# A causal attention block: a score moved within its step, row maxima split in SBUF, some adds on VectorE and part of W1's sums moved into attention

## The chip, the cores and the metric

The kernel runs on one core of one Trainium2 chip. The time is that of the device for one execution, in microseconds (us), as the median of several runs. The hardware profiler records one further execution. The profile names the engines PE (TensorE: matmuls), PEld (its weight loads), DVE (VectorE), ACT (ScalarE), POOL (GpSimd) and SP (SyncE, which here issues most DMAs). "L204" is line 204 of the kernel's file.

## The reference

One block of a diffusion transformer in fp32, for x of 2 x 2048 x 512 and 16 heads of 32 channels:

```python
mod = silu(condition) @ Wada + bada            # shift, scale, gate, for attention and MLP
xm = layernorm(x, g1, be1) * (1 + sc_a) + sh_a
scores = einsum('bhqd,bhkd->bhqk', q, k) * hd ** -0.5
attn = softmax(where(causal, scores, -inf))
x = x + gt_a * ((attn @ v) @ Wproj + bproj)
xm = layernorm(x, g2, be2) * (1 + sc_m) + sh_m
x = x + gt_m * (gelu(xm @ W1 + b1) @ W2 + b2)
```

## The kernel before

The two batches run one after the other. For each there is a QKV phase, an attention phase and a projection; the MLP for both comes last. On the profile's time axis: start and QKV of batch 0 from 0 to 202.4, attention 0 to 734.1, projection 0 to 790, QKV of batch 1 to 972.8, attention 1 to 1500.4, projection 1 to 1559.8, MLP to 2278.1.

**Units and steps.** Attention is cut into 16 units per batch, in the list `units`: a group c of four heads (`HC` = 4, together 128 channels) times a block i of 512 queries (`QB`). A unit has 4 i + 3 steps: a step takes one tile of 128 keys against the 512 queries, and the last two steps hold the diagonal's shorter tiles, so that they are narrow (under 512 wide).

**Maxima first.** Every score is computed twice. First in natural layout (queries on partitions): `bank` (line 463) makes one matmul of 128 queries by up to 512 keys, into a tile called s; DVE then takes its row maximum into mx, by a plain reduction (L484) or, at the diagonal, with the causal mask (L479, followed by a small read of an accumulator). The tiles of s come from a PSUM pool of two banks. When the last score of a unit is out, `split` (line 487) turns the unit's maxima into three bf16 parts, mhl, in five small DVE operations (L501 to L505); the maximum itself and a remainder are kept in the columns of the PSUM tile of the last score. `rows` (line 539) transposes mhl on PE (ps_m, also in a bank of the s pool) and DVE spreads it into fold (L549).

**Then the step.** `scores_t` (line 578) starts the four heads' transposed scores st (keys on partitions) in four further PSUM banks, each with a matmul of sel and fold, which puts minus the maximum there, and adds the product of keys and queries. ACT takes the exponential into e (L620), POOL zeroes what lies above the diagonal (affine_select, L629). Two steps later (`LAG` = 2) PE makes the products o of e and the values vv. For the row sums sm, the e of four steps are first added up by POOL in chains (L650, `add`, line 648), so that PE needs one product with ones for four steps; in the last unit of a batch DVE adds.

**What sets the order.** The scores in natural layout belong to units up to three ahead (`AHEAD`) and wait in `row.todo`. For each step `due` and `count` work out from costs how many, n, are to be issued; `scores_t` places them among the transposed scores: with n over 4 one ahead of the first head, one behind heads 0 and 2 each, one in a bank of the st pool behind head 3, and one more; what is over goes behind the step's products. The order of PE, of ACT's exponentials and of POOL is that of the code (`mm` and `act` keep it); DVE's reductions and the loads may be moved by a scheduler. The pending products are issued by `flush`, which in the last unit stands behind `row.prepare`: that is the step's share of work for the projection, with a matmul ps_rows that turns rows of the gate.

**Loads.** Keys kst and queries qst go to DRAM and come back in another layout; `asked` (line 879) asks for the first ones of a group of tokens in the QKV phase, keys first, on SP's queue.

**Weights.** The MLP's matrices are multiplied by a scheme with seven products in place of eight, at two levels, so W1 and W2 need sums of their blocks, which POOL makes ahead of time. The class `Quarters` makes the 16 pieces of the first level: eight in QKV of batch 0, eight in attention 0 (with `beside` and `among`, line 1150: loads and stores on SP's queue, the sums, L1135, in steps of the diagonal, where POOL has no adds). `FirstLayer` makes W1's second level in QKV of batch 1: seven pieces, each with a load of 1 MB and a store on POOL's own queue and four sums (L1196).

**End of the projection.** `inv_std` (line 222) takes a square root on ACT (rstd2) for the second layernorm behind the last statistics, for either batch. The MLP's matmuls ps_a and ps_b, and ACT's copies c (L1877), follow.

Of the kernel before, what the change touches and what calls it, by code (L numbers as in the profile page):

```python
# [17 lines left out]
P = 128  # L18
# [9 lines left out]
def dit_block_kernel(  # L28
# [283 lines left out]
    class Row:  # L312
# [174 lines left out]
        def split(self, u, mx, s):  # L487

            hl = mhl[u % (AHEAD + 1)][:, :, : 4 * TQ].rearrange(
                "p h (t l) -> p h t l", l=4
            )
            mx = mx.rearrange("p (h t) n -> p h t n", h=HC)
            m, rest = [
                s[:, n * HC * TQ : (n + 1) * HC * TQ].rearrange("p (h t) -> p h t", h=HC)
                for n in range(2)
            ]  # L500
            nc.vector.tensor_reduce(m, mx, axis=AX.X, op=ALU.max)  # L501
            nc.vector.tensor_reduce(hl[:, :, :, 0], mx, axis=AX.X, op=ALU.max)
            nc.vector.tensor_tensor(rest, m, hl[:, :, :, 0], ALU.subtract)
            nc.vector.tensor_tensor(hl[:, :, :, 1], m, hl[:, :, :, 0], ALU.subtract)
            nc.vector.tensor_tensor(hl[:, :, :, 2], rest, hl[:, :, :, 1], ALU.subtract)  # L505
# [11 lines left out]
        def score(self, n, borrow=None):  # L517

            for k in range(n):
                if borrow and k % 2 == 0:
                    s = borrow()
                else:
                    s = ps_sp.tile([P, QB], F32, tag="s", name="s")
                item = self.todo.pop(0)
                u = item[0]
                if self.mx is None:
                    self.mx = bp.tile(  # L530
                        [P, HC * TQ, units[u][1] + 1], F32, tag="mx", name="mx", bufs=3
                    )
                self.bank(*item, s)
                if not self.todo or self.todo[0][0] != u:
                    self.split(u, self.mx, s)
                    self.mx = None
                    self.at += 1
# [26 lines left out]
    def attention_phase(row, beside=None):  # L564
        b, vv, kst, qst = row.b, row.vv, row.kst, row.qst
        with pool(f"att{b}") as ap, pool(
# [7 lines left out]
            def scores_t(u, step, n):  # L574
# [73 lines left out]
            def add(u, dst, x, y):  # L648
                engine = nc.vector if u == len(units) - 1 else nc.gpsimd
# [61 lines left out]
            for u, (c, i) in enumerate(units):  # L711
# [5 lines left out]
                for n_step, tiles in enumerate(steps_of[u]):  # L717
# [82 lines left out]
    class Qkv:  # L800
# [46 lines left out]
        def group(self, g, hp, between, among):  # L847
# [31 lines left out]
            def asked():  # L879
                row.load_keys(0, g)  # L880
                row.load_queries(g)
# [219 lines left out]
    class Quarters:  # L1101
# [8 lines left out]

        def load(self, room, queue=nc.gpsimd):
# [38 lines left out]
        def beside(self, pool_):  # L1150
# [4 lines left out]
            def among(now, slack, last):  # L1155
                if not todo and self.at < FC:
                    todo.extend([(now + 3, "load"), *((now + 6, n) for n in range(4))])
                    if now == 0:
                        todo[0] = (0, "load")
# [5 lines left out]
                if what == "load":  # L1165
                    todo.pop(0)
                    self.load(room, nc.sync)
                    todo[:] = [(now + 3, n) for n in range(4)]
                elif what == "store":
                    todo.pop(0)  # L1170
                    self.store(nc.sync)
                elif slack or last:
                    todo.pop(0)
                    self.make((what,))
# [3 lines left out]
            return among  # L1178

# [25 lines left out]
    class FirstLayer:  # L1205
# [20 lines left out]
        def store(self):  # L1226

            act(nc.gpsimd.dma_start(w1e[self.stored], self.rooms[self.stored % 2]))
            self.stored += 1

    def project_phase(row, psum, between):
# [59 lines left out]
        lo, hi = b * NT, (b + 1) * NT  # L1291
        inv_std(mv2, rstd2, lo, hi, shift2)
# [147 lines left out]
    attention_phase(row, quarters.beside)  # L1440
# [4 lines left out]
    with pool("qkv1") as qp, pool("ps_qkv1", bufs=6, space=PSUM) as ps_mm:  # L1445
# [20 lines left out]
        with pool("hl1") as hp:  # L1466
# [14 lines left out]
            late_loads = range(1, 43, 6)  # L1481
            qkv.run(hp, also)
            assert late.stored == 7

    attention_phase(row)
# [6 lines left out]
    with ExitStack() as mlp:  # L1492
# [692 lines left out]
```

## Time and profile before

| | us |
|---|---|
| median of 3 runs | 2277.54 (2277.3 to 2277.65) |
| profiled execution | 2279.83 |
| its span | 2278.1 |
| PE busy | 2238.0 (98%) |
| DVE busy | 1556.9 (68%) |
| POOL busy | 1317.1 (58%) |
| ACT busy | 980.2 (43%) |
| busiest DVE group: reductions L484 of s | 409.2 in 606 |
| busiest POOL group: adds L650 to a chain | 498.6 in 212 |

The span is the time between the first and the last instruction that the profiler shows. The table of busy times gives the sum over all phases; an engine that is idle for half of the kernel can still be the one that everything waits for in a stretch. A row of the waits lists what one engine waited for, as it can be inferred from semaphores. A row of the groups by line ends with the idle time of the engine ahead of the group's instructions. A row of the timeline has the start, the duration, the engine, the line, the operation with its output and inputs, how many were put together (x2), and in brackets the idle time before and what ended it.

### The profile page before, as it was taken

Reading aid. Unit: us, or ns where it says so; the run is one execution under the profiler, and the core shown is the slowest. Engines: PE = TensorE matmul, PEld = TensorE weight load, DVE = VectorE, ACT = ScalarE, POOL = GpSimd, SP = SyncE. Lnnn points to the kernel's source line nnn. Section 1 sums busy time; section 2 is a strip of 40 time slices with the busy share of each in tenths; the row PEclk is TensorE's granted clock in tenths of the full one; section 3 lists DMA queues with packets and bytes.
Section 4 is the critical chain, followed back from the end, with each engine's and each line's share of the span. In section 5 each row is a group of like instructions: output and inputs, shape, how many; then the busy total and the mean of one; then the engine's idle time right before and its main releaser. Section 6 shows DMA issues by size and latency. Waiting matters only on the chain. (4 is left out here: it accounts for less than half of the span.)

```text
span 2278.1 us, 34363 instructions
## 1 busy us (share of the span) xinstructions
PE 2238.0 (98%) x12429; PEld 1439.8 (63%) x12429; DVE 1556.9 (68%) x3132; ACT 980.2 (43%) x1908; POOL 1317.1 (58%) x1052
## 2 busy tenths in 40 slices
PE   8999999999999999999999999999999999999999
PEld 3676455455544457754555545446888888888887
DVE  3467777777766525677777777555896876877787
ACT  3334555555566134355555555632332242251231
POOL 4362987888894553258788887554764602602510
PEclk9999999999999999999999999999999999999999
DMA  8869226262244778860511404265375654654643
GB/s 272 250 209 249 50 52 156 55 146 73 56 153 148 240 245 295 266 149 24 120 44 46 104 24 136 85 224 202 117 278 203 212 180 151 214 176 153 221 144 120
DMA packets 134147, 355.66 MB, mean 156 GB/s; under 512 B 14497, under 2 KB 33485, under 8 KB 119257
## 3 DMA queue, kind: packets, MB, share of 16 engines
q1 hardware_dynamic: 126112, 305.18, 45.1%
q0 software_dynamic: 7488, 47.74, 5.8%
q8 instruction: 98, 1.61, 0.3%
q14 instruction: 73, 0.59, 0.1%
q10 hardware_dynamic: 376, 0.55, 0.1%
HBM read 253.80 MB, written 107.48 MB: 159 GB/s over the span
## 5 line engine op out<-in xcount | busy, mean ns | idle before, releaser
L620 ACT ACTIVATE e<-st 128x512 f32<-128x512 f32 (+1 forms) x1152 | 572.9, 579 | 404.6 <-PE st L204 347.6
L484 DVE TENSOR_REDUCE mx<-s 128x1 f32<-128x512 f32 x606 | 409.2, 687 | 193.0 <-PE s L204 191.1
L650 POOL TENSOR_TENSOR ee<-ee,e 128x1024 f32<-128x1024 f32 x212 | 498.6, 2383 | 8.1 <-ACT e L620 8.1
L204 PE MATMUL s<-kst,qst 128*128 128x512 f32 (+3 forms) x1028 | 439.0, 430 | 15.1 <-DVE mx L484 8.6
L204 PE MATMUL st<-qst,kst 128*128 128x512 f32 (+3 forms) x1280 | 400.6, 377 | 0.0
L204 PE MATMUL ps_a<-sum,room 128*128 128x256 f32 x1504 | 356.8, 381 | 4.4 <-DVE c L1655 1.5
L204 PEld LDWEIGHTS ps_a<-sum,room 128*128 128x128 f32 x1504 | 280.8, 190 | 53.8 <-issue 6.0
L204 PE MATMUL o<-e,vv 128*32 128x512 f32 (+3 forms) x2560 | 302.9, 538 | 1.7 <-POOL e L629 1.7
L479 DVE CUSTOM_DVE_ANT_0 junk<-s,causal 128x512 bf16<-128x512 f32 (+3 forms) x422 | 206.7, 490 | 114.9 <-PE s L204 107.1
L204 PEld LDWEIGHTS s<-kst,qst 128*128 128x128 f32 x1028 | 193.3, 188 | 137.1 <-issue 44.3
L204 PEld LDWEIGHTS st<-qst,kst 128*128 128x128 f32 x1280 | 229.0, 188 | 63.2 <-issue 33.9
L650 POOL TENSOR_TENSOR ee<-e 128x1024 f32<-128x1024 f32 x84 | 198.2, 2382 | 112.1 <-ACT e L620 112.0
L629 POOL TENSOR_SCALAR_AFFINE_SELECT e<-e 128x256 f32<-128x256 f32 x256 | 103.8, 435 | 125.7 <-ACT e L620 124.2
L204 PEld LDWEIGHTS <-sel 32*128 32x128 bf16 x1152 | 29.2, 91 | 190.0 <-issue 188.0
L1883 POOL TENSOR_TENSOR c<-c,h 128x512 f32<-128x512 f32 x40 | 58.5, 1484 | 154.6 <-ACT c L1881 154.6
L204 PE MATMUL ps_b<-sum,room 128*128 128x256 f32 x608 | 143.6, 379 | 0.0
L204 PEld LDWEIGHTS o<-e,vv 128*32 128x32 f32 x2560 | 62.5, 108 | 100.8 <-issue 80.6
L204 PEld LDWEIGHTS ps_b<-sum,room 128*128 128x128 f32 x608 | 115.0, 190 | 15.4
L204 PE MATMUL ps_v<-wqkv,xmT 128*128 128x512 f32 x256 | 124.7, 600 | 0.0
L204 PE MATMUL st<-fold,sel 32*128 32x512 bf16 (+1 forms) x1152 | 115.3, 372 | 2.6 <-DVE mhl L505 1.2
L484 DVE TENSOR_REDUCE mx<-st 128x1 f32<-128x512 f32 x162 | 111.0, 685 | 2.9 <-PE st L204 0.6
L1528 POOL TENSOR_TENSOR sum<-xm 128x256 f32<-128x256 f32 x16 | 15.5, 972 | 152.8 <-PE ps_a L204 152.8
(236 smaller groups left out, 3276.5 us busy)
## 6 DMA issues: line engine op xcount, KB each, us to landing
qst<-q SPq DMA_DIRECT2D x128, 256.0 KB
room<-w1e SPq DMA_DIRECT2D x28, 1024.0 KB
kst<-k SPq DMA_DIRECT2D x24, 1024.0 KB
room<-w1e SPq DMA_DIRECT2D x28, 768.0 KB
room<-w2e SPq DMA_DIRECT2D x21, 1024.0 KB
q<-hl SPq DMA_DIRECT2D x32, 512.0 KB
k<-hl SPq DMA_DIRECT2D x32, 512.0 KB
room<-w2e SPq DMA_DIRECT2D x21, 768.0 KB
```

Of the source, the lines that this page charges most:

```text
L204: return tc.keep_in_program_order(nc.tensor.matmul(*args, **kw))
L479: nc.vector.tensor_tensor_reduce(junk[:, :w], s[:, :w], causal[:, QB - w :], 1.0, MASKED, ALU.add, ALU.max, m,)
L484: nc.vector.tensor_reduce(m, s[:, :w], axis=AX.X, op=ALU.max)
L620: act(nc.scalar.activation(e[:, h % 2, :w], sts[h][:, :w], AF.Exp))
L629: nc.gpsimd.affine_select(d, d, pattern=[[0, 2], [1, P]], compare_op=ALU.is_ge, fill=0.0, base=0, channel_multiplier=-1,)
L650: act(engine.tensor_tensor(dst, x, y, ALU.add))
L1528: act(engine.tensor_tensor(dst, x, y, ALU.subtract))
L1883: nc.gpsimd.tensor_tensor(c, c, piece_of(base, i, t, pair), ALU.add)
```

## The change

1. In a step with more than four scores that is 512 wide (and not in the first unit), the third score goes behind the fourth transposed score, ahead of the one in the st bank. In narrow steps, and in the first unit, it goes behind the one in the st bank.
2. `split` keeps its parts in an SBUF tile and works in six DVE operations, all reductions, in place of five. It no longer touches the last score's bank.
3. `add` takes DVE as soon as no score is left to do in the batch, in place of in the last unit alone.
4. In the last unit the pending products are issued ahead of `row.prepare`.
5. `asked` asks for queries ahead of keys.
6. Only three of W1's seven second-level pieces are made in QKV of batch 1. The other four are made in attention 1, as eight halves: the new class `FirstHalves` with 32 sums of 128x256, eight loads of 0.5 MB and eight stores on SP's queue, placed by `beside` as W2's are in attention 0.
7. Batch 1's `inv_std` is called in the MLP (first block, k = 3); at its old place stands a small square root.

```diff
-        def split(self, u, mx, s):
+        def split(self, u, mx):
...
-            m, rest = [
-                s[:, n * HC * TQ : (n + 1) * HC * TQ].rearrange("p (h t) -> p h t", h=HC)
-                for n in range(2)
-            ]
-            nc.vector.tensor_reduce(m, mx, axis=AX.X, op=ALU.max)
+            parts = bp.tile([P, HC, TQ, 3], F32, tag="parts", name="parts")
+            nc.vector.tensor_reduce(parts[:, :, :, 0], mx, axis=AX.X, op=ALU.max)
             nc.vector.tensor_reduce(hl[:, :, :, 0], mx, axis=AX.X, op=ALU.max)
-            nc.vector.tensor_tensor(rest, m, hl[:, :, :, 0], ALU.subtract)
-            nc.vector.tensor_tensor(hl[:, :, :, 1], m, hl[:, :, :, 0], ALU.subtract)
-            nc.vector.tensor_tensor(hl[:, :, :, 2], rest, hl[:, :, :, 1], ALU.subtract)
+            for n in range(1, 3):
+                nc.vector.tensor_reduce(
+                    parts[:, :, :, n], hl[:, :, :, n - 1 : n],
+                    axis=AX.X, op=ALU.max, negate=True,
+                )
+                with nc.allow_low_precision("sums of exact parts, rounded when written"):
+                    nc.vector.tensor_reduce(
+                        hl[:, :, :, n], parts[:, :, :, : n + 1], axis=AX.X, op=ALU.add
+                    )
...
-                after = (0, 2) if n > HC else (0, 1)
+                narrow = w < QB or u == 0
...
-                    if h in after and n >= 3 or h >= HC - n and n < 3:
+                    if h < 1 + (n <= HC) and n >= 3 or h >= HC - n and n < 3:
                         row.score(1)
+                if n > HC and not narrow:
+                    row.score(1)
                 if n >= 3:
                     row.score(1, st_bank)
-                    row.score(min(n, HC) - 3)
+                if n > HC and narrow:
+                    row.score(1)
+                if n > 3:
+                    row.score(1)
...
             def add(u, dst, x, y):
-                engine = nc.vector if u == len(units) - 1 else nc.gpsimd
+                engine = nc.gpsimd if row.todo else nc.vector
...
                     row.inverses(u, n_step)
+                    flush(now)
                     if u == len(units) - 1:
                         row.prepare(n_step)
-                    flush(now)
...
             def asked():
+                row.load_queries(g)
                 row.load_keys(0, g)
-                row.load_queries(g)
...
+    class FirstHalves:
...
+        def load(self, room, queue):
+            n, half = self.at // 2, self.at % 2
+            self.at += 1
+            w = room.rearrange("p (n d) -> p n d", n=7)
+            src = w1d[:, n].rearrange("p k (i f) d -> p (k i) (f d)", i=2)
+            act(queue.dma_start(w[:, 2:6], src[:, :, half * 2 * P : (half + 1) * 2 * P]))
+            self.loaded.append((n, half, w))
...
+                room_sum(self.loaded[0][2], 1, step)
...
+            act(queue.dma_start(w1e[n][:, :, half * 2 * P : (half + 1) * 2 * P], w))
...
-        lo, hi = b * NT, (b + 1) * NT
-        inv_std(mv2, rstd2, lo, hi, shift2)
+        if b + 1 < B:
+            inv_std(mv2, rstd2, 0, NT, shift2)
+        else:
+            act(nc.scalar.activation(first, eps, AF.Sqrt))
...
-            late_loads = range(1, 43, 6)
+            late_loads = range(1, 19, 6)
...
-    attention_phase(row)
+    halves = FirstHalves(late.stored)
+    attention_phase(row, beside(halves))
...
             def among(at, k):
+                if (m, at, k) == (0, 0, 3):
+                    inv_std(mv2, rstd2, NT, B * NT, shift2)
```

More of the change, by code (lines that the diff above doesn't have):

```diff
@@ L1148, in store, with beside, start @@
             )
-        def beside(self, pool_):
+    def beside(pieces):
+        def start(pool_):
             room = pool_.tile([P, piece], F32, tag="w7", name="w7")
@@ L1155, in among @@
             def among(now, slack, last):
[L1156 to L1159, printed above, removed]
+                if not todo and pieces.left():
+                    todo.append((now + 3 if now else 0, "load"))
                 elif not todo:
```

26 lines of the change are left out of this document (20 added, 6 removed).

## Prediction

> **What bounds the kernel now.** I read first the table of stretches, cut at the borders of the phases: from, to, length, then the busy time and count of PE, PEld, DVE, ACT and POOL. The second and the fourth stretch of the kernel, attention of batch 0 and of batch 1, matter most here:
>
> ```profile
> 202.40:734.10 531.70, 522.08 (x3682) 263.79 (x3681) 373.61 (x893) 303.33 (x608) 426.52 (x313) 1.00 0.40 103
> ...
> 972.80:1500.40 527.60, 519.57 (x3681) 262.71 (x3680) 373.47 (x893) 302.95 (x607) 404.37 (x281) 1.00 0.32 81
> ```
>
> PE is busy for 98% of both, at a granted clock of 1.00. DVE is busy for 70%, POOL for 80% and 77%. So PE's own sequence is the time, and the change, which leaves the count and the shapes of the matmuls alone, can only win what PE waits. Next come PE's waits, in attention 0 and then in attention 1 (total us, times, longest):
>
> ```profile
> PE s L204 <- DVE mx L484: 5.2, 8, 0.9
> PE o L204 <- POOL e L629: 1.3, 2, 1.1
> PE s L204 <- DVE mx L479: 0.9, 3, 0.4
> PE st L204 <- DVE mhl L505: 0.6, 1, 0.6
> PE ps_rows L204 <- ACT e L620: 0.5, 1, 0.5
> ```
> ```profile
> PE s L204 <- DVE mx L484: 3.4, 6, 0.9
> PE s L204 <- DVE mhl L505: 2.0, 4, 0.6
> PE st L204 <- DVE mhl L505: 0.6, 1, 0.6
> ...
> PE ps_rows L204 <- ACT e L620: 0.5, 1, 0.5
> PE o L204 <- POOL e L629: 0.5, 1, 0.5
> PE s L204 <- DVE mx L479: 0.2, 1, 0.2
> ```
>
> Scores wait 22 times for a maximum or for the split: 5.2 + 0.9 + 3.4 + 2.0 + 0.2 = 11.7 us. These rows are the pool from which the change can draw. The timeline of one such place (start, duration, then the instruction, in brackets the idle time before it) shows how it comes about and that the rows show too little:
>
> ```profile
> 1224.51 0.40 PE L204 MATMUL st<-qst,kst 128*128 128x512 f32 x1
> ...
> 1224.72 0.68 DVE L484 TENSOR_REDUCE mx<-s 128x1 f32<-128x512 f32 x1
> ...
> 1225.32 0.18 DVE L505 TENSOR_TENSOR mhl<-s,mhl 128x16 bf16<-128x16 f32 x1
> 1225.45 0.33 PE L204 MATMUL s<-kst,qst 128*128 128x128 f32 x1 [0.55 <-DVE mx L484]
> ```
>
> The split's L505 still reads a PSUM bank of the s pool. PE's next score into that bank starts at 1225.45, as L505 ends. It is named after L484, but L505 is the last to end. The row says 0.55; the starts are 1225.45 - 1224.51 = 0.94 apart.
>
> The usual distance of two starts is in the next fence, with the first and the last of the third scores of which part 2 speaks:
>
> ```profile
> 203.90 0.40 PE L204 MATMUL s<-kst,qst 128*128 128x512 f32 x1
> 204.13 0.62 PE L204 MATMUL st<-qst,kst 128*128 128x512 f32 x2
> 204.62 0.50 PE L204 MATMUL s<-kst,qst 128*128 128x512 f32 x1
> 204.95 0.40 PE L204 MATMUL st<-qst,kst 128*128 128x512 f32 x1
> ```
> ```profile
> 1418.71 0.63 PE L204 MATMUL st<-qst,kst 128*128 128x512 f32 x2
> 1419.20 0.50 PE L204 MATMUL s<-kst,qst 128*128 128x512 f32 x1
> 1419.54 0.39 PE L204 MATMUL st<-qst,kst 128*128 128x512 f32 x1
> ```
>
> From 203.90 to 204.13 it is 0.23. So the split cost 0.94 - 0.23 = 0.71 there, 0.16 more than the row, and the matmul behind a score that waited starts late too: 0.34 behind it (1419.20 to 1419.54), 0.11 over 0.23. A wait in the table is therefore worth its figure plus some 0.28.
>
> **The change part by part.**
>
> **1. Split in SBUF.** No s bank is read by the split any more, so the program's order has no PE matmul behind it. Four of the 22 waits have no split in front and stay; they stand behind the transposition of the split parts. The first and the last of them:
>
> ```profile
> 210.24 0.50 PE L204 MATMUL s<-kst,qst 128*128 128x512 f32 x1 [0.73 <-DVE mx L484]
> ...
> 1043.33 0.38 PE L204 MATMUL s<-kst,qst 128*128 128x256 f32 x1 [0.23 <-DVE mx L479]
> ```
>
> Each batch has one of either size: 2 x (0.73 + 0.23) = 1.9. That leaves 9.8 us in 18 waits, and 18 x 0.28 = 5.0 beside them: 14.8. What is late next is the reduction that the split still delays on DVE, since six small operations stand ahead of it: I keep 1.5 us for this. **-13.3.** The fold's matmul (st behind L505, 0.6 in each batch) loses its wait too: 2 x (0.6 + 0.28), **-1.8**. The sixth operation adds some 0.2 us to DVE per split (L505 takes 0.18), 32 times, beside PE work, in the 30% in which DVE idles; without this cover it would be 6 us.
>
> **2. Third score.** In the steps with five scores at full width (92 of them, 46 per batch) the third waits a moment for the bank of the first. Two starts at 0.23 would put it 0.46 behind the pair of st; it comes 0.49 behind in both fences, and the next st 0.33 and 0.34 behind it: 0.13 and 0.14 lost. Over all 92 the mean is 0.105, 9.7 us. Behind the fourth st it comes 0.23 later, with the bank free. Two of the steps lie beside a split and are counted above (1.8): **-7.9**. Bounds: 0, if the excess belongs to the score's place whatever stands in front of it, and -9.7. I take the nearer end, because the other scores start at 0.23. In narrow steps the score goes behind the one in the st bank; they show no wait of their own, so nothing.
>
> **3. Queries ahead of keys (QKV of batch 1).** Twin stretches of PE, batch 0 and batch 1:
>
> ```profile
> 105.81 2.74 PE L204 MATMUL ps_v<-wqkv,xmT 128*128 128x512 f32 x6
> ...
> 112.69 0.79 PE L204 MATMUL s<-kst,qst 128*128 128x512 f32 x1
> ```
> ```profile
> 874.55 2.74 PE L204 MATMUL ps_v<-wqkv,xmT 128*128 128x512 f32 x6
> 879.59 0.67 PE L204 MATMUL s<-kst,qst 128*128 128x512 f32 x2 [2.31 <-DMA qst<-q]
> ...
> 885.47 0.80 PE L204 MATMUL s<-kst,qst 128*128 128x512 f32 x1
> ```
>
> 10.92 against 6.88: the query load lands late and PE runs unevenly behind it. The queries now go first on SP's queue, and four of the seven W1 loads and stores leave this phase: **-4.0** (0 to -4.0; what is late next is the key load, which the same scores read).
>
> **4. Adds on DVE, products first.** By the order of the instructions eight adds (four per batch) go from POOL to DVE. POOL's price, from the groups by line, and DVE's, from the timeline:
>
> ```profile
> L650 POOL TENSOR_TENSOR ee<-ee,e 128x1024 f32<-128x1024 f32 x212 | 498.6, 2383 | 8.1 <-ACT e L620 8.1
> ```
> ```profile
> 724.35 1.23 DVE L650 TENSOR_TENSOR ee<-ee,e 128x1024 f32<-128x1024 f32 x1 [0.30 <-POOL e L629]
> ...
> 725.87 2.29 DVE L650 TENSOR_TENSOR ee<-ee,e 128x1024 f32<-128x1024 f32 x1 [0.30 <-POOL e L629]
> ```
>
> POOL loses 8 x 2.38 = 19 us, DVE gains 8 x 1.23 = 9.8 to 8 x 2.29 = 18.3. PE's products then no longer wait for POOL's late masks (1.3 + 0.5): **-1.8**, between -1.8 and +2 by what DVE's two prices leave. The products ahead of ps_rows take its wait, 2 x (0.5 + 0.28): **-1.6**. The Trainium skill says in "SBUF — State Buffer", section "SBUF: two separate sides", that VectorE and GpSimd share one pair of ports as an exclusive lock, so that a VectorE operation with two SBUF inputs and a GpSimd one that reads SBUF exclude each other for a whole instruction. That speaks against moving adds to DVE while POOL still works, and the trace agrees: 2.29 instead of 1.23 at 725.87. By it the term would be about nothing instead of -1.8, since only the adds that meet POOL pay.
>
> **5. W1's sums in attention 1.** Attention 0 has done the same since before, with W2's (the stretch row for L1135 alone), and its stores wait on SP's queue:
>
> ```profile
> 202.40:734.10 531.70, 24.00 (x32) 1.00 0.40 103
> ```
> ```profile
> SPq L1144 <- POOL e L629: 65.3, 7, 31.3
> ```
>
> Attention 0 is 531.7 - 527.6 = 4.1 us longer, of which 0.8 is the larger o row. So 32 sums cost between 0 and 4.1 there, and 24.0 if all lay on the path. I take +2.2, near the middle of what the rows show. The loads and stores go on SP's queue, ahead of query loads, sums and outputs; in attention 0 no PE row waits for a DMA although SP's stores wait 65.3 us, so nothing for them. QKV of batch 1 loses 16 sums and four store-load pairs, on which PE does not wait: nothing.
>
> **6. POOL behind a faster PE.** POOL would work 404.4 - 9.5 + 24.0 = 419 us in some 513 of attention 1, and adds of 2.38 run in chains. Its masks come later against PE: **+2.0** (0 to 6, by the o row of 1.3 and the waits at unit borders becoming frequent).
>
> **7. Statistics of batch 1 in the MLP.** PE's first wait there:
>
> ```profile
> 1564.73 1.97 PE L204 MATMUL ps_a<-sum,room 128*128 128x256 f32 x8 [1.34 <-ACT c L1877]
> ```
>
> In the order of instructions the square root still stands right behind the table load and ahead of the copies, as now: nothing (1.3 if it really moved).
>
> Sum: -13.3 - 1.8 - 7.9 - 4.0 - 1.8 - 1.6 + 2.2 + 2.0 = **-26.2**. The profiled execution took 2279.83: 2253.6. The median of the runs, 2277.54, lies 2.3 below it: **2251**.
>
> **The rivals.** **A. POOL takes over** in the long units, where it has least to spare: PE's products then wait for its masks, and half of attention's -26.4 (parts 1, 2, 4) is given back, 13: 2264. For it: 82% busy after the change. Against it: only 1.8 us of waits for POOL now.
>
> **B. DVE takes over; slower.** The last three scores of a step now follow each other at 0.23, and one reduction takes more:
>
> ```profile
> 1213.61 0.69 DVE L479 CUSTOM_DVE_ANT_0 junk<-s,causal 128x512 bf16<-128x512 f32 x1 [0.70 <-PE s L204]
> 1214.23 0.08 DVE L479 DVE_READ_ACCUMULATOR2_ANT mx<- 128x1 f32 x1
> 1214.23 1.37 DVE L484 TENSOR_REDUCE mx<-s 128x1 f32<-128x512 f32 x2
> ```
>
> If DVE comes out of the five later by one st and one late start, 0.34, and the next step's scores wait for it, 92 x 0.34 = 31 us replace the 7.9 of gain: -26.2 + 7.9 + 31 = +12.7, so 2290. It decides at whether DVE idles ahead of the third. Here it is done with the second at 1214.23 + 0.68 = 1214.9, about when the moved score would end (1215.0): a tie, and DVE idled 0.70 ahead of the step. So I think the delay is covered.
>
> **C. It doesn't do it.** The waits reappear as waits for the reductions, because DVE still runs split and reductions in one queue; only parts 3 and 4 stay, with 5 against them: -4.0 - 3.4 + 2.2 = -5: 2272, and anything less lies within 0.2%.
>
> **How the numbers follow.** Forecast 0.62 (its own range 2245 to 2257: all paybacks gone, -30, or part 2 without gain and part 5 at 4.1), A 0.18, C 0.10, B 0.10. Forecast and A are faster by over 0.2% (4.6 us, about what a measurement of this kernel can tell from no change): 0.80; C counts as the same, since it sits at that edge: 0.10; B slower: 0.10. The range reaches from the forecast's low bound to A with part 5 at its 4.1: 2244 to 2266.
>
> **What would show it.** Right: no wait for the split's lines in the waits of PE, and attention stretches of some 517 and 515 us; third scores 0.23 behind their st; the stretch from the ps_v matmuls at 874.55 to the score at 885.47 in 6.9 us; no row of ps_rows. Wrong: rows of s behind L484 in five-score steps (B), rows of o behind POOL in the long units (A), or rows of the same size behind other reductions next to the splits (C). The MLP's stretch should stay at its length.

## The result and the profile after

The changed kernel took 2264.53 us (median of 6 runs, 2263.53 to 2268.16) against 2277.53 for the kernel before: a ratio of 0.9944, 95% interval 0.9931 to 0.9957. Timed again on another occasion the ratio was 0.9934 (0.9921 to 0.9948). So it is 13 to 15 us faster, about half of the 26 that the prediction had.

The table of stretches for the changed kernel (from, to, length, busy time and count of PE, PEld, DVE, ACT, POOL); the three rows are attention 0, QKV of batch 1 and attention 1:

```profile
201.29:725.70 524.41, 520.50 (x3682) 266.50 (x3681) 379.88 (x911) 302.96 (x608) 420.87 (x309) 1.00 0.41 105
...
782.40:960.20 177.80, 177.11 (x663) 118.28 (x661) 91.46 (x234) 64.18 (x138) 44.99 (x46) 1.00 0.66 206
960.20:1483.90 523.70, 520.02 (x3681) 266.55 (x3680) 379.94 (x911) 302.28 (x607) 422.05 (x309) 1.00 0.39 104
```

Attention 0 is 7.3 us shorter, attention 1 3.9, QKV of batch 1 4.2 (182.0 before). Projection and MLP kept their lengths. The start was 1.1 us shorter, which is no effect of the change. In the profile of the kernel before, the granted clock of TensorE fell to half for 3.4 us there, and again in QKV of batch 1:

```profile
19.70:23.10 3.40, 3.40 (x5) 1.35 (x4) 0.00 (x0) 0.23 (x1) 1.19 (x2) 0.50 1.01 365
879.80:883.20 3.40, 3.40 (x7) 1.75 (x7) 1.56 (x4) 0.00 (x0) 2.48 (x4) 0.51 1.06 346
```

(The clock is the third figure from the end.) In the profiles of the kernels below, the start takes 202.1 to 202.9 us where it has such a stretch and 199.9 to 201.5 where it has none, and the MLP takes 722 in the four that have one there and 718 to 719 in the others. This is why the lengths of the phases, taken from the timeline, tell more here than whole times, and why a stretch at half clock is named below wherever it bears on a length.

PE's waits in attention 0 and in attention 1 of the changed kernel:

```profile
PE o L204 <- POOL e L628: 0.8, 1, 0.8
PE ps_m L544 <- DVE mx L479: 0.8, 1, 0.8
PE s L204 <- DVE mx L484: 0.6, 2, 0.4
PE s L204 <- DVE mx L479: 0.5, 1, 0.5
```
```profile
PE o L204 <- POOL e L628: 0.9, 2, 0.8
PE ps_m L544 <- DVE mx L479: 0.8, 1, 0.8
PE s L204 <- DVE mx L484: 0.6, 2, 0.4
...
PE s L204 <- DVE mx L479: 0.5, 1, 0.5
```

Nearly all that the prediction wanted gone is gone: no row of the split, none of ps_rows, 2.2 us of scores waiting in place of 11.7. Of these 2.2, 1.7 are the four waits that the prediction let stand (1.9 before). New is ps_m: in either phase, a transposition of split parts waits 0.8 us for a maximum. PE's idle time fell by 9.6 - 3.9 = 5.7 us in attention 0 and by 8.0 - 3.7 = 4.3 in attention 1. But PE's busy time, from which the prediction wanted as much again (the 0.28 per wait and the late starts of the third scores), fell by 1.6 only in attention 0 and rose by 0.5 in attention 1. What was missing lies there, between starts that the rows of PE's waits do not show.

### The profile page after: what moved, and what is told of

The parts are those of the page before. It is cut to its first block, busy times and chain, and to the rows that moved or that the text cites. A ratio compares the mean times of both kernels' runs of the same rounds, so it can differ in the third digit from the quotient of the medians.

```text
span 2261.8 us, 34418 instructions
## 1 busy us (share of the span) xinstructions
PE 2233.7 (99%) x12429; PEld 1445.4 (64%) x12429; DVE 1570.8 (69%) x3172; ACT 979.6 (43%) x1909; POOL 1305.9 (58%) x1052
## 4 chain that ended last, share of the span: by engine, by line
PE 88%; DVE 7%; issue 3%; POOL 1%; ACT 1%; DMA 0%; SPq 0%; DVEq 0%; ACTq 0%; POOLq 0%
PE st L204 17%; PE ps_a L204 15%; PE o L204 11%; PE s L204 10%; PE ps_b L204 7%; PE ps_v L204 5%; PE ps_o L204 5%; PE sm L204 4%; PE ps_u L204 4%; PE ps_c L204 4%; PE ps_w L204 3%; PE ps_qk L204 2%; DVE sum L1570 1%; PE ps_xt L212 1%; DVE h L1697 1%
## 5 line engine op out<-in xcount | busy, mean ns | idle before, releaser
L654 POOL TENSOR_TENSOR ee<-ee,e 128x1024 f32<-128x1024 f32 x204 | 480.5, 2389 | 8.0 <-ACT e L619 8.0
L204 PE MATMUL s<-kst,qst 128*128 128x512 f32 (+3 forms) x1028 | 433.0, 426 | 3.7 <-DVE mx L484 1.1
L204 PE MATMUL st<-qst,kst 128*128 128x512 f32 (+3 forms) x1280 | 380.7, 377 | 0.0
L628 POOL TENSOR_SCALAR_AFFINE_SELECT e<-e 128x256 f32<-128x256 f32 x256 | 109.7, 466 | 139.6 <-ACT e L619 139.2
L204 PEld LDWEIGHTS ps_b<-sum,room 128*128 128x128 f32 x608 | 115.0, 190 | 15.4
```

Source lines behind the costliest of these rows:

```text
L204: return tc.keep_in_program_order(nc.tensor.matmul(*args, **kw))
L628: nc.gpsimd.affine_select(d, d, pattern=[[0, 2], [1, P]], compare_op=ALU.is_ge, fill=0.0, base=0, channel_multiplier=-1,)
L654: act(engine.tensor_tensor(dst, x, y, ALU.add))
```

## The experiments

The theory at the start: PE's waits went as worked out, but what is won comes back in the same phase, on POOL (rival A), whose masks then come late. The rivals: DVE, with its reductions in one queue, gives it back (B and C), or the third score never had anything to win. All lengths are from the profiles of the kernels, all ratios from timed runs beside the kernel before.

| kernel | ratio to before (95%) | attention 0 | QKV 1 | attention 1 |
|---|---|---|---|---|
| before | 1 | 531.6 | 182.0 | 527.5 |
| changed | 0.9944 (0.9931 to 0.9957) | 524.4 | 177.7 | 523.7 |
| changed, again (after_again) | 0.9934 (0.9921 to 0.9948) | 524.1 | 177.8 | 523.8 |
| split_only | 0.9976 (0.9967 to 0.9986) | 529.1 | 182.6 | 525.1 |
| third_only | 1.0009 (1.0000 to 1.0018) | 531.9 | 180.9 | 529.6 |
| w1_only | 0.9996 (0.9987 to 1.0005) | 531.6 | 177.7 | 530.9 |
| add_flush | 0.9987 (0.9978 to 0.9996) | 529.7 | 182.2 | 526.3 |
| split_third | 0.9974 (0.9961 to 0.9986) | 528.9 | 181.0 | 525.0 |
| no_w1 | 0.9953 (0.9940 to 0.9967) | 524.2 | 181.1 | 522.5 |
| no_split | 0.9983 (0.9974 to 0.9992) | 529.6 | 177.9 | 529.3 |
| no_third | 0.9933 (0.9920 to 0.9945) | 524.8 | 177.8 | 524.5 |
| late_sums | 0.9928 (0.9916 to 0.9940) | 524.0 | 177.8 | 523.7 |
| late_adds | 1.0492 (1.0478 to 1.0507) | 588.3 | 177.8 | 589.2 |
| half_reduce | 0.9896 (0.9882 to 0.9910) | 520.6 | 176.8 | 520.1 |
| before_half_adds | 0.9954 (0.9937 to 0.9970) | 524.8 | 181.1 | 523.6 |
| split_half_adds | 0.9921 (0.9902 to 0.9940) | 519.4 | 183.1 | 520.2 |
| after_half_adds | 0.9876 (0.9857 to 0.9894) | 518.0 | 177.8 | 519.2 |
| masks_first | 0.9893 (0.9878 to 0.9908) | 520.1 | 177.8 | 519.7 |
| masks_mid | 0.9890 (0.9874 to 0.9907) | 520.1 | 177.8 | 519.6 |

### The parts by themselves

**split_only** is the kernel before with this edit alone:

```diff
-                    self.split(u, self.mx, s)
+                    self.split(u, self.mx)
...
+            parts = bp.tile([P, HC, TQ, 3], F32, tag="parts", name="parts")
```

> The kernel before with only the split moved to SBUF. Prediction's working (a split wait is worth its row and 0.28 us): 13.3 + 1.8 = 15 us faster, 0.9934 of before, no PE wait for the split's lines left. Rival 1 (the rows alone count, and half of the reductions behind the split stay late): about 8 us faster, 0.9965. Rival 2 (POOL's masks take over as soon as PE is faster): 5 us or less, with more PE waits of o for POOL than the 1.8 us before.

Attention became 2.5 and 2.4 us shorter, in all 4.9 where 15 were expected. A single split shows both sides. In the timeline of the kernel before, a step runs from its fold matmuls to the next ones:

```profile
414.83 0.29 PE L204 MATMUL st<-fold,sel 32*128 32x256 bf16 x4
...
416.72 0.50 PE L204 MATMUL s<-kst,qst 128*128 128x512 f32 x1 [0.93 <-DVE mx L484]
...
418.45 0.40 PE L204 MATMUL st<-fold,sel 32*128 32x512 bf16 x4
418.77 0.50 PE L204 MATMUL s<-kst,qst 128*128 128x512 f32 x1
...
422.09 0.40 PE L204 MATMUL st<-fold,sel 32*128 32x512 bf16 x4
```

The same two steps in split_only:

```profile
411.21 0.29 PE L204 MATMUL st<-fold,sel 32*128 32x256 bf16 x4
...
412.00 0.40 PE L204 MATMUL s<-kst,qst 128*128 128x512 f32 x1
...
413.63 0.83 PE L204 MATMUL st<-fold,sel 32*128 32x512 bf16 x4
414.39 0.50 PE L204 MATMUL s<-kst,qst 128*128 128x512 f32 x1
...
417.71 0.40 PE L204 MATMUL st<-fold,sel 32*128 32x512 bf16 x4
```

The first step shrank from 3.62 to 2.42, by 1.20 = 0.93 + 0.27: the wait is gone with its 0.28 of hidden cost. But the second grew from 3.64 to 4.08. Its four folds now take 0.76 up to the first score (413.63 to 414.39) in place of 0.32: the last of them needs the st bank in which the score ahead of the last was put, and DVE, with the split's operations among its reductions, gets to that score late:

```profile
413.64 0.20 DVE L502 TENSOR_REDUCE mhl<-parts 128x16 bf16<-128x48 f32 x1
413.75 0.28 DVE L479 CUSTOM_DVE_ANT_0 junk<-st,causal 128x128 bf16<-128x128 f32 x1
413.96 0.08 DVE L479 DVE_READ_ACCUMULATOR2_ANT mx<- 128x1 f32 x1
```

It ends at 414.04. Over the whole of attention 0, ten steps shrank by over 0.15 us, by 7.2 together, and ten grew, by 4.9; in attention 1 ten shrank by 5.7 and seven grew by 3.3. The largest growth is in the last unit, before and in split_only:

```profile
687.38 2.13 PE L204 MATMUL o<-e,vv 128*32 128x384 f32 x16 [1.12 <-POOL e L629]
```
```profile
681.55 2.99 PE L204 MATMUL o<-e,vv 128*32 128x384 f32 x16 [2.12 <-POOL e L628]
```

PE now comes to these products 2.1 us ahead of POOL's mask. They also take longer, since the granted clock is 0.51 from 682.1 to 685.5; this costs 1.3 us in this step and the next. So 12.9 us were won and 8.2 came back, behind POOL in part and behind DVE in part. How much belongs to which is measured below.

**third_only** has this edit alone:

```diff
+                if n > HC and not narrow:
+                    row.score(1)
                 if n >= 3:
                     row.score(1, st_bank)
```

> The kernel before with only the third score moved. Prediction's working: 8 to 10 us faster (0.9960), since 92 starts no longer lose 0.105 us. Rival (the excess belongs to the score behind a pair wherever it stands): 0 to 3 us faster, 0.9990 to 1.0000, with the excess at the moved score or at the one behind it.

Nothing was won: the phases are 0.2 and 2.0 us longer, and so is the whole (2 us, with an interval from 0 to 4). Of the 2.0 us, 1.6 are one step in which the clock was at half for 3.4 us:

```profile
978.16:983.39 5.23, 5.23 (x29) 2.08 (x30) 2.76 (x6) 1.32 (x4) 0.81 (x2) 0.67 1.03 215
```

The same step takes 5.23 in after_half_adds, with the same clock, and 3.5 to 3.7 in all others. Without it the two phases are 0.7 us longer. The rival was right that there is nothing to win, but not on the reason, which the next group shows.

**w1_only** moves W1's four pieces alone; keys stay ahead of queries.

```diff
-            late_loads = range(1, 43, 6)
+            late_loads = range(1, 19, 6)
...
-    attention_phase(row)
+    halves = FirstHalves(late.stored)
+    attention_phase(row, beside(halves))
```

> The kernel before with only W1's four pieces moved into attention 1 (keys still ahead of queries). Theory that the sums stand ahead of masks on POOL: attention 1 is 3 to 4 us longer (about 531, as attention 0), with PE waits of o for POOL in the units' last steps. Prediction's working: 2.2 longer. QKV of batch 1: 4 us shorter if W1's traffic held up the query load, unchanged at 182 if the order of the loads did. So 1.0015 or 0.9997 of before.

Attention 1 got 3.4 us longer and QKV of batch 1 4.3 shorter, without the new order of the loads. **no_w1** is the other side, the changed kernel without the move and with queries first:

```diff
-            late_loads = range(1, 19, 6)
+            late_loads = range(1, 43, 6)
```

> The changed kernel with W1's seven pieces back in QKV of batch 1, and no sums in attention 1. If the four moved pieces cost attention 1 the 3.4 us by which it gained less than attention 0 (3.9 against 7.3), and queries ahead of keys alone mend QKV: 3.4 us faster than the changed kernel, 17 us faster than before (0.9927), attention 1 about 520. If QKV's 4.2 us came from the smaller traffic of W1: QKV is back at 182 and the time equals that of the changed kernel (0.9944).

QKV of batch 1 is at 181.1 again. Its timeline has the wait that the query load had caused, with another name:

```profile
867.26 2.74 PE L204 MATMUL ps_v<-wqkv,xmT 128*128 128x512 f32 x6
869.43 0.80 PE L204 MATMUL s<-kst,qst 128*128 128x512 f32 x1
871.89 0.30 PE L204 MATMUL s<-kst,qst 128*128 128x128 f32 x1 [1.66 <-DVE mx L484]
```

and the changed kernel doesn't have it:

```profile
865.98 2.74 PE L204 MATMUL ps_v<-wqkv,xmT 128*128 128x512 f32 x6
...
872.83 0.79 PE L204 MATMUL s<-kst,qst 128*128 128x512 f32 x1
```

Its stretch takes 6.85 us, as the twin of batch 0 does (6.88). So it is W1's pieces that held up this phase; whether by their loads and stores or by POOL's sums, these runs do not separate. The order of the loads won nothing: with all of W1 in this phase and no stretch at half clock, it takes 180.9 to 181.1 with keys first (third_only, split_third, before_half_adds) and 181.1 with queries first (no_w1). The 182.0 of the kernel before has 3.4 us at half clock behind its wait of 2.3 us for the query load. So W1's move is worth 3.3 of the 4.2, and about one is this stretch, which the changed kernel has not. (That PE waits for the key load at 871.89 is read, not shown: the named reduction had ended a microsecond before.) In attention 1 the four pieces cost 1.2 us when the other parts are there (no_w1 against the changed kernel), 3.4 when they are not.

**add_flush** has the two edits of the prediction's part 4 alone:

```diff
-                engine = nc.vector if u == len(units) - 1 else nc.gpsimd
+                engine = nc.gpsimd if row.todo else nc.vector
...
+                    flush(now)
                     if u == len(units) - 1:
                         row.prepare(n_step)
-                    flush(now)
```

> The kernel before with the adds on DVE once the scores are done and the products ahead of the projection's preparation. Prediction's working: 1.8 + 1.6 = 3.4 us faster (0.9985). If these parts alone hold the 7.3 us by which the changed kernel without W1's move beats split and third score (4.8 and 2.6 in the two phases): 7 us faster (0.9969). If most of that is only the split's late masks mended: 3 to 4 us.

2.0 and 1.2 us, in all 3.2, where 3.4 were worked out. The sum met by luck, as three steps of each phase make it up. The first step of the last unit, where PE waited for POOL's mask, is 2.3 and 1.6 us shorter, 3.8 for the 1.8 of the prediction. The step with ps_rows is 0.6 shorter in both, 1.2 for 1.6. And the last step is 0.8 longer in both; in the changed kernel, too, it takes 8.28 in place of 7.42. DVE's adds and POOL's operations meet there, and in the changed kernel it is POOL's that takes longer (before, then changed), so that the masks behind it start later:

```profile
725.81 1.27 POOL L457 TENSOR_TENSOR kst<-kst,bgate 128x512 f32<-128x512 f32 x1
```
```profile
716.46 2.24 POOL L457 TENSOR_TENSOR kst<-kst,bgate 128x512 f32<-128x512 f32 x1
```

### Parts together, and left out

**split_third** puts the split and the third score together (the diffs of split_only and third_only).

> The kernel before with the split in SBUF and the third score moved, and nothing else. If the two only add up (-2.5 and +0.25 in attention 0, -2.4 and +2.0 in attention 1): 2.6 us faster than before, 0.9988, and the waits for POOL of 2.1 us at the last unit stay. If they help each other: 8 us faster, 0.9965.

They neither add up in full nor help much: 0.3 us more than the split alone. Against no_w1, which has part 4 as well, 4.8 and 2.6 us are missing, 7.3 for edits that alone bring 3.2: with DVE's adds the wait of the last unit, 2.1 us long in split_only, is gone too, and so is the stretch at half clock behind it (1.3). **no_split** says the same of the split:

```diff
-                    self.split(u, self.mx)
+                    self.split(u, self.mx, s)
```

> The changed kernel with the split back in the last score's PSUM bank. Theory that POOL gives back what the split wins, and that the adds on DVE mend a part of this: the split is worth 4 to 5 us more than alone (5), so 8 to 10 us slower than the changed kernel, attention 0 and 1 at about 528.5 and 528. Prediction's working: 15 us slower. If it simply adds up: 5 us slower.

5.2 and 5.6 us longer than the changed kernel. The split is worth 10.8 in company and 4.9 alone (6.2 without the stretch at half clock).

**no_third** has the third score at its old place, in a kernel that is otherwise the changed one (**after_again** was timed beside it).

```diff
-                if n > HC and not narrow:
-                    row.score(1)
```

> The changed kernel, timed beside the next three. Both theories: 0.9944 of before.

> The changed kernel with the third score back behind the third transposed one. Prediction's working: 8 us slower than the changed kernel (0.9978). Theory that the move gains nothing, because later places of the step lose what the third wins (attention 0 +0.25 and attention 1 +2.0 us with the move alone): equal to the changed kernel or up to 2 us faster (0.9940). Theory that the move works only with the split in SBUF: about 5 us slower (0.9966).

0.4 and 0.8 us longer than the changed kernel, and the same in time. Of the 100 steps of one key tile in which the score moves, 69 have the same length within 0.1 us, 23 are 0.2 shorter in the changed kernel and 8 0.2 longer. (The first of a unit's two diagonal steps is 384 + 128 = 512 wide, so that it is not narrow, and the score moves there as well: in 26 more steps, of which 23 kept their length.) One of the 69 in no_third, with the weight loads (PEld) of its third and fifth score:

```profile
365.52 0.40 PE L204 MATMUL st<-fold,sel 32*128 32x512 bf16 x4
...
367.13 0.19 PEld L204 LDWEIGHTS s<-kst,qst 128*128 128x128 f32 x1 [0.29 <-DVE mx L484]
...
367.72 0.19 PEld L204 LDWEIGHTS s<-kst,qst 128*128 128x128 f32 x1 [0.18 <-DVE mx L484]
...
369.15 0.39 PE L204 MATMUL st<-fold,sel 32*128 32x512 bf16 x4
```

and in the changed kernel:

```profile
364.22 0.40 PE L204 MATMUL st<-fold,sel 32*128 32x512 bf16 x4
...
366.04 0.28 PE L204 MATMUL s<-kst,qst 128*128 128x256 f32 x1
...
366.42 0.19 PEld L204 LDWEIGHTS s<-kst,qst 128*128 128x128 f32 x1 [0.19 <-DVE mx L484]
366.42 0.49 PE L204 MATMUL s<-kst,qst 128*128 128x512 f32 x1
...
367.85 0.40 PE L204 MATMUL st<-fold,sel 32*128 32x512 bf16 x4
```

Both take 3.63. The third score at 366.04 indeed waits no more. But the fifth comes 0.38 behind it, its weights loaded only when DVE is through with the second, and the products behind the fifth start 0.43 behind it instead of 0.33. With two banks a score can't start ahead of the end of the reduction of the one two before it in the pool, and DVE needs 0.69 us for one of 512; which of them waits is a matter of place.

**half_reduce** tests that on DVE's side. The unmasked maxima are taken over half of the keys, so that half of the scores are left out of them:

```diff
-                nc.vector.tensor_reduce(m, s[:, :w], axis=AX.X, op=ALU.max)
+                nc.vector.tensor_reduce(m, s[:, : w // 2], axis=AX.X, op=ALU.max)
```

> The changed kernel with the unmasked row maxima taken over half of a score's keys only (the other half left out), so that a reduction takes about 0.42 in place of 0.69 us on DVE. Theory that the moved score's wait went on to the last score of the step, which needs the bank that DVE has not yet read: the exposed starts at the last scores and behind them go, some 3 us per attention phase, and the late folds with them, 8 us faster than the changed kernel in all. Rival (PE's own cost of changing between matmuls): no change in attention.

3.8 and 3.6 us shorter than the changed kernel. DVE's reductions do bind here, as the theory says, by 7.3 us of attention. With a reduction at 0.42 us, PE's starts of folds, of last scores and of what follows scores came earlier by 5.6 us per phase, of which 2.5 between the folds; 1.9 came back in the products, whose weight loads now wait 10.9 us for POOL in either phase, in place of 8.2 and 8.4.

### What POOL costs

**late_sums** moves W1's and W2's sums behind a unit's last masks:

```diff
-                elif slack or last:
-                    todo.pop(0)
-                    pieces.make((what,))
-                    if what == 3:
-                        todo.append((now + 1, "store"))
+                elif slack:
+                    pieces.make(range(4))
+                    todo[:] = [(now + 1, "store")]
...
-                        among(now, n_step >= i * TQ, u + 1 == len(units))
+                        among(now, last and u + 1 < len(units) and units[u + 1][1] > 0, u + 1 == len(units))
```

> The changed kernel, but a piece's four W1 (and W2) sums come together, behind a unit's last masks and only where the next unit's first step has no masks. If the 3.4 us that W1's sums cost attention 1 are products waiting for masks that stand behind a sum: attention 1 back at 520.5 and attention 0 also 2 to 3 us shorter (522), so 5 to 6 us faster than the changed kernel (0.9920 of before). If it is POOL's sum of work that counts: no change, 0.9944.

No change in length: the units' last steps got up to 0.7 us shorter, and in the units behind, whose adds now started 3 us later, steps got up to 1.5 longer. The sums in front of the masks were a true wait, and not the limit.

**late_adds** gives DVE one of the two adds in front of the masks:

```diff
                     elif i and n_step == i * TQ:
-                        add_to(u, chain, es)
+                        add(u, chain[0], chain[0], es[0])
+                        act(nc.vector.tensor_tensor(chain[1], chain[1], es[1], ALU.add))
```

> The changed kernel, but in each unit the second of the two adds ahead of the masks (the first diagonal step's) is DVE's: 24 adds in all, 2.4 us earlier masks. Theory that POOL, with its masks behind the last adds, gives back what the split won: up to 3 us per attention phase faster, 0.9915 of before, products no longer drawn out behind POOL's masks. Rival (DVE cannot spare 1.3 us in that step either): the scores' reductions come late instead, no change or slower, 0.9940 to 0.9965.

126 us slower than the changed kernel (2390.68), far outside what either theory said. The reading: this add waits for POOL, as the row names it until the mask of the e that it adds, which stands behind POOL's earlier adds; and DVE stands still meanwhile with the reductions queued behind it. PE's waits in attention 0, and one of the places (the line numbers of this kernel are shifted):

```profile
PE s L204 <- DVE mx L479: 30.1, 8, 7.1
PE s L204 <- DVE mx L484: 17.3, 4, 7.6
```
```profile
236.09 2.34 POOL L654 TENSOR_TENSOR ee<-ee,e 128x1024 f32<-128x1024 f32 x1
236.17 3.35 DVE L786 TENSOR_TENSOR ee<-ee,e 128x1024 f32<-128x1024 f32 x1 [3.08 <-POOL e L628]
...
240.18 0.58 PE L204 MATMUL s<-kst,qst 128*128 128x256 f32 x1 [5.05 <-DVE mx L484]
```

That is not the whole of it. Of the 64 us by which attention 0 grew, 46 are idle time of PE; the other 18 are in its busy time, 538.1 us in place of 520.5. The matmuls behind the long waits run slower, and the granted clock of the phase is 0.94, against 1.00 in the changed kernel; behind the wait shown it is 0.50 for 6.8 us:

```profile
202.67:790.96 588.29, 538.12 (x3682) 273.28 (x3681) 418.74 (x921) 303.98 (x608) 406.81 (x299) 0.94 0.37 94
238.40:245.20 6.80, 5.03 (x20) 2.47 (x21) 4.45 (x8) 0.59 (x2) 3.83 (x7) 0.50 0.01 2
```

So this run doesn't tell the theories apart. It tells that POOL is that far behind.

To put a price on that, three kernels have chain adds over half of the queries (half of the row sums left out). POOL's 212 adds to a chain then take 266.5 us in place of 498.6. DVE's 28 adds to a chain, which lie in the last units, are halved as well (0.76 us in place of 1.29):

```diff
                 for t, e in zip(chain, es):
+                    t, e = t[:, :, : QB // 2], e[:, :, : QB // 2]
                     add(u, t, t, e)
```

**before_half_adds** is the control:

> The kernel before with the adds to a chain over half of the queries only (the other half of the row sums is left out), so that POOL has some 125 us less to do in each attention phase. The control: PE waited 1.8 us for POOL, so 2 to 4 us faster at most (0.9985), and attention 0 some 2 us shorter.

The control itself is the surprise: 6.8 and 4.0 us shorter. Of these 10.8 us, 1.4 in either phase lie in its last step, where the adds are DVE's; the other 8.0 are POOL's. So much did POOL cost PE before the change already, where PE's waits showed 1.8. The waits of the weight loads do show it. In the kernel before, attention 0 and attention 1:

```profile
PEld o L204 <- POOL e L629: 8.4, 23, 1.6
```
```profile
PEld o L204 <- POOL e L629: 5.5, 15, 0.9
```

and in the control, attention 0:

```profile
PEld o L204 <- POOL e L629: 1.7, 7, 0.3
```

**split_half_adds** has the split on top:

> The same halved adds with the split in SBUF and nothing else. Theory that POOL's late masks give back what the split wins: the steps with a split keep their 7.2 and 5.7 us and the steps behind them lose nothing, so 12 to 13 us faster than the control (attention 0 and 1 shorter by 7 and 6). Rival (the reductions behind the split, on DVE, give it back): 5 us faster than the control, as with the full adds.

5.5 and 3.4 us shorter than the control, 8.8 together, against 4.9 with full adds. The growth in the last unit (2.3 and 1.0, with the 1.3 at half clock) is gone. What stays are the small growths in the steps behind a split, 1.7 and 2.3 for those over 0.15: 4 us, which don't depend on POOL's adds. So of the 8.2 that came back, about half is POOL's, and the other half is most likely DVE's, as the split shown above has it: neither theory alone.

**after_half_adds** is the changed kernel with the same:

> The changed kernel with the same halved adds. Theory that POOL gives back: 4 to 5 us per attention phase faster than the changed kernel, 8 to 10 in all (0.990 of before). Rival (DVE): no more than the control gains over before, 2 us.

6.4 and 4.5 us shorter than the changed kernel, 10.9, and 12.4 without the step at half clock that this run has in attention 1. Of this, 2.3 in either phase lie in the last step, which the change had made longer. The other 7.9 are POOL's adds: what they cost is the same after as before (8.0). With the split alone POOL was worse, as the wait of 2.1 us shows; that the eight adds which went to DVE made up for this, and for W1's sums, is likely but not tested by itself.

### A version that is faster than both

The halved adds point to the order on POOL: in a unit's first diagonal step, two adds of 2.4 us stand ahead of the masks of the next two steps, while their sum is needed two steps later than the masks. **masks_first** puts these adds behind the unit's last masks, **masks_mid** between those of the second and the last diagonal step.

```diff
                     elif i and n_step == i * TQ:
-                        add_to(u, chain, es)
+                        if row.todo:
+                            behind.append((u, chain, es))
+                        else:
+                            add_to(u, chain, es)
...
+                    if behind and last:
+                        add_to(*behind.pop())
```

> The changed kernel, but POOL's last two adds of a unit go behind the unit's last masks (while scores are left to do), so that no mask but the first step's stands behind an add. Halving the adds showed that POOL costs PE some 11 us, in the changed kernel as before. If that is masks behind these adds: up to 11 us faster than the changed kernel, about 0.990 of before. Rival (the adds two steps later hold e buffers, and the exponentials wait for them): the gain is lost or turned, 0.994 to 1.000, with waits of ACT for POOL.

> The same with the two adds between the masks of the second diagonal step and those of the last one. Theory of masks behind adds: about half of the gain, as only one of two mask steps is freed, 4 to 6 us faster than the changed kernel, 0.992. Rival (buffers): less harm than with the adds behind the last masks.

Both are some 9 us faster than the changed kernel (2255.27 and 2254.93 us; 0.989 of before against 0.993 to 0.994), 4.2 and 4.0 of it in the two phases of either. The weight loads of the products wait half as long for POOL, in attention 0 of the changed kernel and of masks_first:

```profile
PEld o L204 <- POOL e L628: 8.2, 24, 1.7
```
```profile
PEld o L204 <- POOL e L628: 4.5, 9, 1.7
```

The gain lies in the same six steps of either phase in which after_half_adds wins outside the last one, and each gains the same within 0.02 us (1.3 us in one, 0.4 to 1.0 in the others; 4.5 in all). So what POOL's adds cost in these steps was the order of two of them. masks_mid doesn't gain half but the same; freeing the second step's masks is what counts. The rival's sign, ACT waiting for POOL's adds, did grow, from 4.3 us in attention 1 to 6.5 and 5.2, but cost nothing that shows.

## Why the prediction was half right

The forecast stood at 26 us and 13 to 15 were measured; the phases of attention and QKV give 15.4 in the profiles. The time of rival A came out (2264), and that is luck: its sign, rows of o behind POOL, is 0.8 and 0.9 us, and most of what was missing is not POOL's. Of the signs of the forecast all came but one, the length of attention. (Two sums of the prediction do not follow from its terms. Attention by them is 1037 us in all, 1059.3 - 22.2, and not 517 + 515. Part 2 without gain and part 5 at 4.1 give 2261, and not 2257, as the upper end of the forecast's own range.)

- **Part 2 failed, and with it most of the gap.** The third score was put at -7.9, by "I take the nearer end, because the other scores start at 0.23". Measured: -0.3 (split_third against split_only) to -1.2 (no_third), and +0.7 alone (+2.3 with the step at half clock). The excess at the third score was real and did go. But the reason given, a bank that is free 0.23 later, looked at this score alone. The fifth score inherits the same wait, since DVE's reductions and the two banks set the pace. The prediction named the end 0 and ruled it out for the wrong reason; rival B's question (does DVE idle ahead of the moved score?) was the right one, but had only a loss in view, not a wait that is handed on.
- **Part 1 was right in kind and too large.** All waits named went, and 0.28 beside a wait was right where nothing else was late (1.20 for a row of 0.93). But 12.9 us came out of the steps, where 14.8 + 1.8 = 16.6 were worked out, since some scores beside a split wait for a reduction instead (1.6 us of such rows in split_only). And what the delayed reductions cost in the next step was put at 1.5; it is 4 (split_half_adds).
- **Part 3 had the size right (4.2), in part by luck.** It named two reasons, and only one holds: W1's pieces are worth 3.3, the order of the loads nothing. The rest is that PE "runs unevenly" behind the late load in the kernel before, which is its stretch at a clock of 0.51.
- **Part 4** was right in its sum by itself (3.2 for 3.4), with terms that were off and made up for each other: POOL's masks -3.8 for -1.8, ps_rows -1.2 for -1.6, and +1.6 where DVE's adds meet POOL. It was worth more together with the split, 7.3 (1.3 of it the clock), because it removes waits of the last unit that the split would have made.
- **Part 5** lay within its bounds: 1.2 in company, 3.4 alone, for 2.2.
- **Part 6** took POOL's price from PE's waits, 1.8 us, and it was 8.0. It was not the change that was mispriced by this but the place where the time lay: it stays as it was, 7.9.
- **Part 7** was right. ACT's copies still hold the MLP's first wait of this kind, 1.36 us after and 1.34 before.

Rival C, in which the waits reappear behind the reductions, describes part 2 and about half of what came back in part 1. It had been given 0.10 as one case for all parts, where the truth was C for one part and some of another.

## What to carry to other kernels

A wait of a few hundred ns on this pool of two banks was set by the engine that empties them; moving one matmul behind another handed the wait to the next one that uses the pool, so look for the next user before pricing the gain. PE's waits alone understated what POOL cost, 1.8 us for 8.0: read the waits of the weight loads too, and measure by halving the other engine's work. Look at the granted clock of a stretch before a microsecond or two of it is explained otherwise. And on an engine that works in order, what is needed first should be issued first: two adds behind the masks instead of ahead of them were worth as much as the larger parts of this change.

## What was not expected of the hardware

Of the 24 adds that late_adds gives to DVE, 15 took 3.35 to 3.38 us; DVE's 32 adds to a chain in the last units took 1.27 in the mean. The 15 began just behind the start of an add of POOL: in the place shown above, POOL's runs from 236.09 to 238.43 and DVE's, begun at 236.17, ends at 239.52, 1.09 behind it. The Trainium skill, "SBUF — State Buffer", section "SBUF: two separate sides", describes a lock by which a VectorE operation with two SBUF inputs and a GpSimd operation that reads SBUF exclude each other for a whole instruction; this agrees with it. In the changed kernel the adds met POOL rarely: its 36 adds to a chain on DVE took 1.33 in the mean.

The granted clock fell to half behind short waits as well, but not behind each. In QKV of batch 1, with all of W1 there, it did so behind waits of PE of 2.3, 2.5, 2.6 and 3.1 us (before, add_flush, split_only, split_half_adds), and not behind those of 2.2, 2.3 and 2.8 (third_only, split_third, before_half_adds). What decides it stays open.
